# SyncE issues three of a band's sixteen window loads instead of two

## The chip, the cores and the metric

The kernel runs on one core of one Trainium2 chip. The metric is the device time of one execution in microseconds, the median of several. The profile is of one execution of the same kernel, and its span (first to last instruction) is a little shorter than that execution's own time.

## The reference: what is computed

The input is 32 images of 256 channels, 32 x 32 pixels, in f32. Two layers follow one another, each adding its result to its input:

- Layer 0: group norm over 32 groups of 8 channels; values and weights brought to a 16-bit float format; a 3 x 3 convolution from 256 to 256 channels; its result brought to the same format; a bias.
- Layer 1, an "involution": group norm `g = gn(x)` again; a 1 x 1 convolution of g to 64 channels, batch norm and relu; a second 1 x 1 convolution of the result to 16 x 49 values a pixel. These are weights: for each of 16 groups of 16 channels and each pixel, the output is the sum over a 7 x 7 window of g, each place weighted by that pixel's own weight for that place.

```
w = einsum('oc,bchw->bohw', w2, y) + b2      # 784 weights a pixel
out = einsum('bgkhw,bgckhw->bgchw', w, patches)   # k runs over 7 x 7 places
x = x + out
```

## The kernel before

**Tiling.** Images go through one after the other. The work of an image in layer 1 is cut into K = 4 bands of TR = 8 rows; so there are 128 bands. A band has two sides (left and right half of the columns). Instead of gathering the window of each output pixel, the kernel scatters each input pixel: a matrix with one row for each input pixel of the band and one column for each place of an output that it reaches, multiplied with the pixels' channels, adds all outputs of the window in PSUM. That matrix is banded, which gives `band` its name: three tiles (NBAND = 3) of 128 partitions, used in turn, zero outside the band. Partition p of the tile holds, for one row and one column pair, 7 columns of 160 weights.

**How a band comes about** (all in f32):

1. `weights` (L403): matmuls on PE (L411) make the 784 weights of 4 rows of pixels into PSUM tiles `pw`; DVE adds the bias and writes them to the ring `w_sb` (L435).
2. `scatter` (L465): SyncE stores the weights of a band to a DRAM tensor `wd` in the shape that the loads need, seven transfers of 160 KB (L476), one for each column of the window: four in a first part, three in a second.
3. `load_bands` (L478): the band is read from `wd` in sixteen transfers (L497), one for each column pair j (column j of the left half and its mirror image of the right half). Each writes 8 partitions (j, j + 16, ...) and two sides, so 16 rows. A row is 7 x 160 + 8 elements, 4,512 bytes; pairs 0, 1 and 2 lie at the edge of the image, where `cut` = 3, 2 and 1 columns of the window fall outside, and have rows of 2,592, 3,232 and 3,872 bytes (40.5, 50.5 and 60.5 KB a transfer, the others 70.5).
4. `sums` (L508): 128 matmuls a band on PE (L522), 64 a side, into `acc`; DVE adds the result to the image (L538), and SyncE stores it (L543).

Beside this, `front` (L284) works on a later image: group norms on ACT and DVE, the 3 x 3 convolution on PE (L332) with its eviction on DVE (L346, L348), the 1 x 1 convolution (L377) and the transposes of the pixels (L396). SyncE also loads the images (L106).

**Order.** The order is written out by hand: a loop over steps n (L556), 16 steps an image, 4 a band. At each step it calls the pieces that are due: `sums` of a side every second step; `weights` 18 steps before the sums of their image's place (LEAD); the two parts of `scatter` one and two steps after the weights that complete a band; `load_bands` 9 steps before the band's first sums. Each engine runs its instructions in that order.

**Two queues.** In `load_bands`, line L496 picks the engine that issues a transfer: SyncE for the pairs in BY_SYNC (L66), GpSimd for all others. ORDER (L67) gives the order of the sixteen. SyncE's queue thus holds, in order: seven scatters a band, two of the band's loads (in most bands between the first and the second part of a scatter), two stores and two image loads an image. GpSimd's queue holds nothing but the other fourteen loads of each band, after some memsets at the start. The first load of a band on each queue waits until the sums of the band that last used this tile (three bands before) are done, and until the scatter has landed in `wd`. Each queue uses eight DMA semaphores in turn, and a transfer waits for the one that used its semaphore last, that is, the eighth before it.

Of the kernel before, what the change touches and what calls it, by code (L numbers as in the profile page):

```python
# [62 lines left out]
ROW = S * WPIX  # L63
WR = 4
NBAND = 3
BY_SYNC = (0, 1)  # L66
ORDER = (0, 4, 8, 12, 2, 5, 9, 13, 3, 1, 6, 10, 14, 7, 11, 15)  # L67
NPIX = 6
RING = 32
# [9 lines left out]
def tile_quant_conv_then_involution(  # L79
# [398 lines left out]
    def load_bands(b, k):  # L478
# [3 lines left out]
        for i, j in enumerate(ORDER):  # L482
# [12 lines left out]
            )  # L495
            queue = nc.sync if j in BY_SYNC else nc.gpsimd  # L496
            queue.dma_start(to, src)  # L497
# [140 lines left out]
```

## Time and profile before

| | before |
|---|---|
| three timed runs | 1355.0, 1355.05, 1357.66 us; median 1355.05 |
| the profiled execution | 1344.24 us, its span 1342.5 us |
| PE busy | 1253.6 us (93%) |
| GpSimd busy | 1014.4 us (76%), 980.3 of it in 1,792 band loads of 0.549 us |
| SyncE's band loads | 256 |
| DMA, mean rate | 270 GB/s, 361.85 MB |
| queue of SyncE | 229.38 MB, 56.8% of 16 engines |
| queue of GpSimd | 128.28 MB, 33.9% of 16 engines |
| mean granted clock of TensorE | 0.982 |

How to read it: "busy" is the time in which an engine works on instructions; for GpSimd the issue of a DMA counts, since it writes the descriptors itself; for SyncE no issue counts as busy. A wait row tells which engine and line stood idle, what it was released by, the total in us, the number of times and the longest. A wait that ends with a DMA is for its landing. "issue" is a wait for nothing that the profile shows. Where the text speaks of records, it is of the single instructions, semaphore counts and DMA packets of the same trace: a transfer's landing is the last count on its semaphore before that semaphore is used again.

### The profile page before, as it was taken

The page shows a single profiled execution, that of the slowest core. Times are in us where ns is not written, and L with a number is a line of the kernel's source. Part 1 is how long each engine was busy: PE and PEld are TensorE (multiplying, and loading weights), DVE is VectorE, ACT ScalarE, POOL GpSimd, SP SyncE. Part 2 cuts the span into 40 slices and gives each one's busy share as a digit, 9 for nine tenths or more (in the row PEclk, how much of TensorE's full clock was granted, in tenths as well). Part 3 has the DMA queues.
Part 4 walks back from the last instruction along what each step waited for, and adds up shares of the span by engine and source line. Part 5 has one row for each costly group of instructions (what it writes and reads, how often), then busy time and mean ns, then how long its engine had stood idle before and what let it go on. Part 6 is the DMA issues. An engine that isn't in the chain of part 4 may idle for free.

```text
span 1342.5 us, 65799 instructions
## 1 busy us (share of the span) xinstructions
PE 1253.6 (93%) x27648; PEld 763.7 (57%) x27648; DVE 818.8 (61%) x2539; ACT 733.3 (55%) x1731; POOL 1014.4 (76%) x1818
## 2 busy tenths in 40 slices
PE   5899999999999999999999999999999999999665
PEld 2356566565555655556655556666555566556454
DVE  3466666565666665656665666766666666666442
ACT  5775656455656556556545655655556564553300
POOL 9067878777787778777778787788777877788785
PEclk9999999999999999999999999999999999999987
DMA  6089999999999999999999999999999999999995
GB/s 228 11 237 295 271 293 293 279 266 281 272 286 282 291 285 270 283 263 280 293 282 283 270 288 282 293 297 296 281 288 275 277 284 290 271 281 266 278 274 166
DMA packets 360724, 361.85 MB, mean 270 GB/s; under 512 B 75056, under 2 KB 304752, under 8 KB 359152
## 3 DMA queue, kind: packets, MB, share of 16 engines
q1 hardware_dynamic: 278512, 229.38, 56.8%
q0 software_dynamic: 81920, 128.28, 33.9%
q8 instruction: 220, 3.60, 1.1%
q14 instruction: 72, 0.59, 0.1%
HBM read 176.60 MB, written 180.76 MB: 266 GB/s over the span
## 4 chain that ended last, share of the span: by engine, by line
PE 60%; DMA 23%; POOL 7%; issue 3%; ACT 3%; DVE 2%; SPq 1%; POOLq 0%; DVEq 0%; ACTq 0%
PE pc L332 25%; PE acc L522 19%; DMA band<-wd 17%; PE pw L411 11%; POOL band L497 7%; DMA wd<-w_sb 6%; PE pt L396 3%; PE py L377 3%; ACT junk L214 1%; SPq L476 1%; DVE w_sb L435 1%; DMA x<-in_x 1%; ACT xn L273 0%; SPq L497 0%; ACT xq L273 0%
## 5 line engine op out<-in xcount | busy, mean ns | idle before, releaser
L497 POOL DMA_DIRECT2D band<-wd x1792 | 980.3, 549 | 315.7 <-DMA band<-wd 182.0
L435 DVE TENSOR_TENSOR w_sb<-pw,late_sb 128x224 f32<-128x224 f32 (+7 forms) x1280 | 330.4, 322 | 419.5 <-PE pw L411 419.2
L332 PE MATMUL pc<-xq,wq 128*128 128x496 f16 (+3 forms) x2304 | 535.2, 379 | 20.3 <-ACT xq L273 18.3
L522 PE MATMUL acc<-band,pixels 64*32 64x190 f32 (+1 forms) x16384 | 426.6, 332 | 51.8 <-DMA band<-wd 42.7
L522 PEld LDWEIGHTS acc<-band,pixels 64*32 64x32 f32 x16384 | 304.7, 107 | 159.7 <-issue 81.1
L332 PEld LDWEIGHTS <-wq 128*128 128x128 f16 x2304 | 206.7, 98 | 316.1 <-issue 102.7
L411 PE MATMUL pw<-late_sb,y 64*32 64x224 f32 (+1 forms) x8192 | 288.9, 333 | 10.8 <-issue 9.4
L538 DVE TENSOR_TENSOR x<-acc,x 128x380 f32<-128x380 f32 (+1 forms) x512 | 262.0, 512 | 32.2 <-PE acc L522 23.2
L411 PEld LDWEIGHTS pw<-late_sb,y 64*32 64x32 f32 x8192 | 186.5, 106 | 38.1 <-issue 21.0
L400 ACT COPY pixels<-pt 128x512 f32<-128x512 f32 x128 | 73.7, 576 | 228.6 <-PE pt L396 228.6
L214 ACT ACTIVATE junk<-x 128x512 f16<-128x512 f32 (+1 forms) x192 | 146.4, 763 | 14.7 <-DVE x L348 12.2
L214 ACT ACTIVATE junk<-x,mean 128x1024 f16<-128x1024 f32 x128 | 147.1, 1149 | 4.3
L245 ACT ACTIVATE s<-back,eps 128x2 f32<-128x2 f32 x64 | 18.9, 296 | 178.6 <-DVE back L230 178.6
L346 DVE TENSOR_SCALAR q<-pc 128x512 f16<-128x512 f32 x128 | 87.2, 681 | 17.6 <-PE pc L332 17.6
L273 ACT ACTIVATE xn<-x,off,rstd 128x512 f32<-128x512 f32 x128 | 96.2, 800 | 0.0
L348 DVE SCALAR_TENSOR_TENSOR x<-q,early_sb,x 128x512 f32<-128x512 f16 x128 | 94.2, 736 | 0.3
L396 PEld LDWEIGHTS pt<-ident,xn 128*128 128x128 f32 x512 | 63.9, 142 | 26.3 <-issue 2.5
L396 PE MATMUL pt<-ident,xn 128*128 128x128 f32 x512 | 78.0, 275 | 0.1
L273 ACT ACTIVATE xq<-x,off,rstd 128x1024 f16<-128x1024 f32 x64 | 75.7, 1227 | 0.0
L235 ACT ACTIVATE mean<-back 128x2 f32<-128x2 f32 x64 | 12.6, 196 | 101.4 <-DVE back L230 101.4
L377 PE MATMUL py<-xn,early_sb 128*64 128x512 f32 x256 | 62.2, 606 | 0.9 <-ACT xn L273 0.9
L224 DVE STREAM_TRANSPOSE across<-sums 128x32 f32<-128x32 f32 x128 | 26.3, 205 | 33.6 <-ACT junk L214 32.4
(40 smaller groups left out, 369.3 us busy)
## 6 DMA issues: line engine op xcount, KB each, us to landing
wd<-w_sb SPq DMA_DIRECT2D x896, 160.0 KB
band<-wd POOLq DMA_DIRECT2D x1664, 70.5 KB, 4.6
x<-in_x SPq DMA_DIRECT2D x64, 512.0 KB
out<-x SPq DMA_DIRECT2D x64, 512.0 KB
band<-wd POOLq DMA_DIRECT2D x128, 60.5 KB, 4.6
band<-wd SPq DMA_DIRECT2D x128, 50.5 KB
band<-wd SPq DMA_DIRECT2D x128, 40.5 KB
band<-in_w SPq DMA_DIRECT2D x2, 1152.0 KB
```

The lines of the kernel that those rows point to most:

```text
L214: nc.scalar.activation(junk[:, n0:n1], src[:, h, n0:n1], func, bias=bias, accum_out=self.sums[:, i : i + 1])
L273: nc.scalar.activation(dst, src, AF.Identity, bias=self.off[:, one], scale=self.rstd[:, one])
L332: nc.tensor.matmul(pc.rearrange("p (r c) -> p r c", c=W)[:, r0 - nt * RT : r1 - nt * RT, c0:c1], wq[:, kh, k, mh * P : (mh + 1) * P], xq[: ...
L346: nc.vector.tensor_scalar(q, pc, F16_MAX, -F16_MAX, ALU.min, ALU.max)
L348: nc.vector.scalar_tensor_tensor(xt[:, mh, cols], q, bias_sb[:, mh : mh + 1], xt[:, mh, cols], ALU.add, ALU.add)
L377: nc.tensor.matmul(py[i * CR : (i + 1) * CR], w1_sb[:, kh, :], px[:, :, i], start=kh == 0, stop=kh == CH - 1,)
L396: nc.tensor.transpose(pt[:, i, h * P : (h + 1) * P], xn[:, h, (m + i) * P : (m + i + 1) * P], ident)
L411: nc.tensor.matmul(pws[i][t * TW : (t + 1) * TW, : dj.stop - dj.start, r], y_sb[b % 2][half, (r0 // 2 + r) * W : (r0 // 2 + r + 1) * W], w ...
L435: nc.vector.tensor_tensor(to, of[:, :, d0:d1], bias[:, :, d0:d1], ALU.add)
L497: queue.dma_start(to, src)
L522: nc.tensor.matmul(at[t * TW : (t + 1) * TW, h, :, f - top : l - top], px[p, a, v * GC : v * GC + TW], of[:, :, a, f - top : l - top, v], ...
L538: nc.vector.tensor_tensor(x_at, of, x_at, ALU.add)
```

## The change

Pair 2 of each band, until now the fourth of GpSimd's fourteen transfers, goes to SyncE's queue. Since ORDER stays as it is, SyncE issues pair 0, pair 2, pair 1 in this order, and GpSimd the thirteen others in the order that they had. Nothing else in the program changes; the same bytes go to the same places.

```
-BY_SYNC = (0, 1)
+BY_SYNC = (0, 1, 2)
 ORDER = (0, 4, 8, 12, 2, 5, 9, 13, 3, 1, 6, 10, 14, 7, 11, 15)
...
             queue = nc.sync if j in BY_SYNC else nc.gpsimd
             queue.dma_start(to, src)
```

More of the change, by code (lines that the diff above doesn't have):

```diff
@@ L65 @@
 NBAND = 3
-BY_SYNC = (0, 1)
+BY_SYNC = (0, 1, 2)
 ORDER = (0, 4, 8, 12, 2, 5, 9, 13, 3, 1, 6, 10, 14, 7, 11, 15)
```

## The prediction

> **What bounds the kernel now.** I read the page from the top, then the waits by engine in two stretches (100 to 1195 us, where all stages run, and 1195 us to the end, where only the last bands are left), then the DMA records one by one. Columns of the first rows: busy us (share of the span) and count; in the group row: busy us, mean ns of one | idle us before, what ended most of it.
>
> ```profile
> PE 1253.6 (93%) x27648; PEld 763.7 (57%) x27648; DVE 818.8 (61%) x2539; ACT 733.3 (55%) x1731; POOL 1014.4 (76%) x1818
> ...
> DMA  6089999999999999999999999999999999999995
> ...
> PE 60%; DMA 23%; POOL 7%; issue 3%; ACT 3%; DVE 2%; SPq 1%; POOLq 0%; DVEq 0%; ACTq 0%
> ...
> L497 POOL DMA_DIRECT2D band<-wd x1792 | 980.3, 549 | 315.7 <-DMA band<-wd 182.0
> ```
>
> PE looks like the bound at 93%, yet a quarter of the chain is DMA and POOL. The group row is the one to take apart: GpSimd spends 0.548 us on each of 14 transfers a band, 7.67 us, and waits for the rest. The waits say for what (us in total, times, longest). First POOL and PE from 100 to 1195 us:
>
> ```profile
> POOL band L497 <- DMA band<-wd: 166.0, 210, 2.9
> POOL band L497 <- issue: 49.4, 65, 3.2
> POOL band L497 <- DMA wd<-w_sb: 21.9, 23, 3.1
> POOL band L497 <- PE acc L522: 3.0, 2, 2.8
> ```
> ```profile
> PE acc L522 <- DMA band<-wd: 13.7, 11, 2.7
> PE pw L411 <- issue: 8.5, 14, 1.1
> PE acc L522 <- issue: 3.6, 5, 1.2
> ```
>
> GpSimd waits mostly for its own earlier transfers. The records show why: its transfers use eight semaphores in turn, and each issue waits until the transfer eight before has landed. Mean time from issue to landing is 4.7 us; eight issues take 4.4 us; so whatever is above that is a stall. It hardly ever waits for a free band (PE acc, 3.0 us). I matched issues, landings and sums band by band (bands 4 to 111): GpSimd starts a band 0.33 us after it ended the one before, but 8.0 us after the band was free and 3.4 us after its scatter had landed; at least 0.63 us always lies between that landing and the start. So **GpSimd is the tight server**: its period is 7.67 busy + 2.2 waiting = 9.9 us, the kernel's own. PE is close behind: its first sums of a band start 1.9 us in the mean after the last transfer has landed, and at 0.16 us when it was waiting.
>
> The other end of the run, 1195 us to the end, the same two engines, and beneath them the busy time by stretch (PE, PEld, DVE, ACT, POOL; then clock, DMA share, GB/s):
>
> ```profile
> PE acc L522 <- DMA band<-wd: 29.0, 11, 4.6
> ```
> ```profile
> POOL band L497 <- DMA band<-wd: 14.3, 25, 1.2
> ```
> ```profile
> 900.00:1100.00 200.00, 194.83 (x4415) 118.62 (x4415) 127.73 (x397) 115.81 (x276) 154.00 (x282) 1.00 0.97 286
> ...
> 1195.00:1330.00 135.00, 104.92 (x2799) 73.83 (x2797) 68.39 (x204) 31.07 (x70) 112.20 (x206) 0.88 0.90 260
> ```
>
> In the last stretch POOL is busy 112 of 135 us, PE 105, and PE waits 29 us for bands: there the run goes at GpSimd's pace. In the steady part PE is busy 1065.9 of the 1095 us (the six stretches of this view), idle 29.1, 13.7 of it by name for bands.
>
> **The change, part by part.** Per band, one GpSimd issue (pair 2, 60.5 KB) goes; SyncE issues it between pairs 0 and 1.
>
> *GpSimd.* Gone: 0.548 us of issue, and its share of the waits for landings. Those are 166.0 us in the steady part's 110 bands, 1.5 a band, 0.11 a transfer. So 0.66 us a band. If the waits stay as they are in all, 0.55; if the unnamed waits go in proportion too (another 49.4/110/14 = 0.03), 0.69. I take 0.66. GpSimd alone would be 128 x 0.66 = 84 us shorter: that is capacity, not gain, since PE is next.
>
> *The last stretch.* GpSimd issues bands 112 to 127 from 1183.3 to 1330.6 us, 9.21 us a band, and the end follows its last issue by 12 us. 16 x 0.66 = **-10.5 us**, little lying beside it, as PE has 30 us free there.
>
> *The steady part.* What is late next is PE. Its waits for bands, 13.7 us in 11 waits, are 1.2 us each; a GpSimd that gains 0.66 us a band up to the 2.8 us (3.4 - 0.63) that the scatter's landing leaves would cover most. Bounds: nothing, if SyncE gives it all back; all of PE's 29.1 us, if the unnamed waits were bands too. I take the named row, **-13.7**.
>
> *SyncE.* A third load of 16 rows of 3,872 bytes. Rows near it: pair 0 takes 0.70 us of issue in the mean (0.58 median), pair 1, next in line behind it, 0.88 (longest 1.58). I take 0.9 a band, as a load behind a load. Behind it on the queue stand pair 1, then in three bands of four the three scatters of the next part (one of which may follow a store), and GpSimd's next band waits for these. In one band of four the x load follows, which waits 2.9 us for a store's landing anyway: free there. SyncE's waits, 100 to 1195 us:
>
> ```profile
> SPq L476 <- DVE w_sb L435: 80.7, 55, 5.1
> SPq L106 <- DMA out<-x: 77.1, 27, 4.1
> SPq L476 <- DMA wd<-w_sb: 34.5, 54, 2.2
> SPq L497 <- DMA wd<-w_sb: 18.1, 31, 1.2
> ```
>
> Waits for DVE and PE, which a longer queue eats before anyone notices, add up to about 147 us (80.7 and some fifteen smaller rows), 1.3 a band; with the x load's free band, 1.5. So 0.9 fits, with 0.6 left. The scatters land up to 0.9 us later, covered by the 2.8 us of mean slack; but a quarter of the bands have under 1.15 us of it. In the 23 bands where GpSimd waits for the scatter today, the way from scatter to sums changes by +0.9 - 0.66 = +0.24 us, 5.5 us. I take **+2** of it, as not all of them reach PE, bounds 0 and +5.5.
>
> *No new wait for the band itself.* Pair 2 needs what pairs 0 and 1 need, and SyncE's last load of a band lands 3.8 to 14.9 us before GpSimd's last (median 9.3), so it isn't the last to come. The eight-in-turn limit holds on SyncE too: 10 issues a band become 11, at 5.2 us to landing 11 x 5.2/8 = 7.2 us of 9.9. The named slot waits (34.5 + 18.1, part of both being other waits on a scatter) would grow by a tenth, 5 us, inside the 0.6 left.
>
> *The DMA engines.* They are full by the digits, but the records overlap on one engine (a 4.5 KB packet takes 174 ns alone, 600 with the other queue's 640-byte packets between), so 97% isn't a limit reached: 40 us stretches run from 258 to 298 GB/s, and the number of GpSimd issues in them goes against their landing time (correlation -0.63), less against the GB/s (-0.37); landing time itself hardly follows the GB/s (+0.28). Pair 2 on GpSimd is 8 packets of 7,744 bytes at 418 ns, 3.3 us of engine time; from 2,592 bytes at 132 ns and 3,232 at 150, 16 packets of 3,872 are some 169 ns each, 2.7 us: a gain of 0.6 in 158 engine-us, 0.4%. Against it: SyncE's loads of 8 partitions signal from eight engines only (18,544 four-byte packets = 16 x 1031 + 8 x 256), so those eight get 0.34 us more each and all lose 0.21: +0.13 us in 9.9. I take nothing for both; bounds -0.4% and +1.3%, -5 and +17 us.
>
> *A rule against it.* The Trainium skill ("DMA: Bandwidth & Descriptors", on why a DMA increments its semaphore by 16) says that a transfer's engine count divides its outermost dimension, and that SyncE's take the lowest-numbered engines; the count of eight agrees with the row above, which engines no run shows. By it all three loads sit on the same half, and the +17 end would be the likelier. The same page, "Issuing engines are not separate DMA queues", grants such a split the issue time alone: 0.55 a band in place of 0.66, 8.8 us in the last stretch in place of 10.5.
>
> **Sum:** -10.5 - 13.7 + 2 = -22 us. The profiled execution took 1344.24 us (span 1342.5, 1.7 around it), so 1322 by its own scale; the median of the three timed runs is 1355.05, 0.8% above, and the same -22 gives **1333**.
>
> **Rivals.**
> 1. *Hidden in the steady part.* PE is busy over 97% there, and its other waits move in when bands come earlier. Only the last stretch is gained: 1355 - 10 = 1345. For it: only 13.7 us by name. Against: images run at 37.8 to 42.4 us each, so some do lose to something.
> 2. *All of PE's gap closes.* The fastest images, 38.0 us with PE at 50.0 of 50, against a mean of 39.7: 27 x 1.7 = 46, and 10 at the end: 1299.
> 3. *It doesn't relieve GpSimd.* Landing times grow with the load on eight engines until its waits take back the 0.66 us: that needs 0.66 x 8/13 = 0.4 us more on 4.7. Time 1355.
> 4. *Slower: SyncE's queue becomes the bound.* Place: the three scatters behind the loads. It decides above 1.5 us of SyncE time a band, its slack. Price: at pair 1's longest, 1.58, plus a third of a slot wait (0.5 us each), 1.75: 0.25 x 110 = 27 us, less the 10 of the end: +17, 1372. For it: issues between 0.30 and 2.64 us show that this queue backs up. Against: the means.
>
> **How the numbers follow.** Likeliest 0.43 (1318 to 1345); rival 1 0.14; rival 2 0.07; rival 3 0.10; rival 4 0.26. Faster by over 0.2% (about what a measurement here can tell): 0.43 + 0.14 + 0.07 = 0.64; same 0.10; slower 0.26. The range runs from 1304, short of rival 2, to 1371, into rival 4 and past the +17 of the eight engines.
>
> **What would show it.** Right: 13 GpSimd issues a band at 0.548; its start after the scatter's landing shrinks from 3.4 us and its waits for the scatter rise; PE's waits for bands fall below 5 us in the steady part and by some 10 at the end; SyncE's wait for DVE w_sb falls from 80.7 towards 10 and its third load takes about 0.9. Wrong: GpSimd's landing time at 5.1 or more (rival 3), SyncE's waits for DVE at zero with issues over 1 us and GpSimd waiting for scatters above 60 us (rival 4).

## The result, and the profile after

The changed kernel takes 1371.12 us (median of four runs, 1369.83 to 1376.16) against 1356.36 us (four runs) before: ratio 1.0128, 95% interval 1.0085 to 1.0170. It is **slower**, by 1.3%, which is some 17 us (15 between the two medians), where 22 us less were forecast. The profiled execution after took 1376.16 us (span 1373.7), 32 more than the profiled one before. The two profiled executions thus lie 2.4% apart, about twice the measured change: differences between their rows tell where the time went, and overstate how much.

The page first: the rows that answer to those shown of the kernel before.

```profile
PE 1254.4 (91%) x27648; PEld 763.9 (56%) x27648; DVE 819.7 (60%) x2539; ACT 735.8 (54%) x1731; POOL 943.1 (69%) x1690
...
DMA  6189989999999999999999999998999999999996
...
PE 65%; DMA 17%; POOL 4%; issue 4%; DVE 3%; SPq 3%; ACT 3%; POOLq 0%; DVEq 0%; ACTq 0%
...
L497 POOL DMA_DIRECT2D band<-wd x1664 | 909.1, 549 | 418.0 <-DMA wd<-w_sb 173.8
```

GpSimd is busy 71 us less, as planned, 128 issues fewer at 0.549 us. But its idle time rose from 316 to 418 us, and what ends most of it has changed: no longer its own transfers (`band<-wd`), but the scatters (`wd<-w_sb`). The waits of GpSimd from 100 to 1195 us (us in total, times, longest) say the same:

```profile
POOL band L497 <- DMA band<-wd: 147.4, 174, 3.1
POOL band L497 <- DMA wd<-w_sb: 123.1, 63, 5.7
POOL band L497 <- issue: 37.0, 54, 2.2
POOL band L497 <- PE pw L411: 12.8, 7, 4.1
POOL band L497 <- PE acc L522: 7.5, 4, 3.7
```

Its waits for its own landings fell by 19 us (166.0 before), its waits for scatters rose by 101 us (21.9 before). PE in the same stretch, then PE and GpSimd from 1195 us to the end:

```profile
PE acc L522 <- DMA band<-wd: 27.1, 17, 3.1
PE acc L522 <- issue: 11.3, 11, 2.5
PE pw L411 <- issue: 9.6, 8, 3.9
```
```profile
PE acc L522 <- DMA band<-wd: 18.4, 6, 4.7
```
```profile
POOL band L497 <- DMA band<-wd: 15.2, 20, 2.1
POOL band L497 <- DMA wd<-w_sb: 11.9, 9, 3.3
```

PE waits for bands twice as long in the steady part as before (13.7) and 11 us less at the end (29.0), where its unnamed waits (`acc` for "issue") rose from 2.5 to 12.0 us; so its waits there are no shorter in all, though this stretch is also some 30 us longer. The busy time by stretch (PE, PEld, DVE, ACT, POOL; clock, DMA share, GB/s) has the share of the DMA engines lower, 0.94 in place of 0.97, and the rate too, 274 in place of 286 GB/s; so nothing here points at a fuller DMA system:

```profile
900.00:1100.00 200.00, 187.91 (x4209) 116.34 (x4211) 124.13 (x386) 112.14 (x265) 138.60 (x254) 0.99 0.94 274
```

And SyncE, 100 to 1195 us:

```profile
SPq L106 <- DMA out<-x: 55.5, 26, 3.6
SPq L476 <- DMA wd<-w_sb: 49.8, 72, 3.2
SPq L497 <- DMA wd<-w_sb: 28.9, 45, 1.4
SPq L476 <- DMA x<-in_x: 20.0, 24, 2.0
SPq L476 <- DVE w_sb L435: 15.7, 26, 3.1
```

Its wait for DVE's weights, the largest of the waits that the prediction counted as slack, is down from 80.7 to 15.7 us; its waits for landings other than the stores' are up. From the records, band by band (bands 4 to 111, means in us; e15 is an experiment below):

| | before | after | e15 |
|---|---|---|---|
| period of GpSimd | 9.92 | 10.25 | 9.90 |
| its issues of one band, waits between them included | 9.59 | 8.75 | 8.69 |
| its gap between bands | 0.33 | 1.49 | 1.19 |
| landing time of its transfers | 4.74 | 4.89 | 4.77 |
| scatter landed to its first issue | 3.38 | 1.58 | 1.38 |
| share of bands in which that is under 0.8 | 12% | 70% | 60% |
| scatter: first part's end to second part's start, median, bands 0 / 1 / 2 / 3 of an image | 2.0 / 2.1 / 2.3 / 0.1 | 3.1 / 2.7 / 3.2 / 0.1 | 1.8 / 1.5 / 2.5 / 0.1 |
| first scatter issue to last landing, the same | 11.6 / 10.5 / 12.7 / 10.4 | 13.2 / 11.6 / 14.5 / 9.8 | 12.0 / 10.5 / 13.0 / 9.6 |
| period in the last 16 bands | 9.21 | 9.01 | 8.78 |

GpSimd gains 0.84 us inside a band and loses 1.16 between bands. The two rows on the scatter show where: SyncE's loads stand between the two parts of the scatter in bands 0 to 2 of an image, and not in band 3. With three of them the second part starts 0.7 to 1.2 us later there, the scatter takes 1.1 to 1.8 us longer from its first issue to its last landing, and GpSimd starts within 0.55 to 0.72 us of its landing (medians, bands 0 to 2). In band 3, where no load stands between, GpSimd still has 4.0 us.

In the mean over bands 0 to 2 a scatter takes 13.08 us from its first issue to its last landing, in place of 11.79. Of the 1.29 us more, 0.46 are the issue of the loads that stand between, 0.25 the scatters' own issue, 0.46 the waits in between, and 0.12 the landing of the last. The profiles of the experiments below agree: 12.5 and 12.8 us in e5 and e7, which also have a third load in this place; 11.8 in e1, e14 and e15, which have two there; 11.2 with one (e4); and 10.9 with none (e3). With pair 2 on ACT, two stand there as well, and it is 12.0 in e2 and e6, 11.8 in e13 and 12.4 in e16.

### The profile page after: what moved, and what is told of

Its sections match the earlier page's. It is cut to its first block, busy times and chain, and to the rows that moved or that the text cites. A ratio compares the mean times of both kernels' runs of the same rounds, so it can differ in the third digit from the quotient of the medians.

```text
span 1373.7 us, 65862 instructions
## 1 busy us (share of the span) xinstructions
PE 1254.4 (91%) x27648; PEld 763.9 (56%) x27648; DVE 819.7 (60%) x2539; ACT 735.8 (54%) x1731; POOL 943.1 (69%) x1690
## 4 chain that ended last, share of the span: by engine, by line
PE 65%; DMA 17%; POOL 4%; issue 4%; DVE 3%; SPq 3%; ACT 3%; POOLq 0%; DVEq 0%; ACTq 0%
PE pc L332 26%; PE acc L522 22%; PE pw L411 12%; DMA band<-wd 12%; DMA wd<-w_sb 5%; POOL band L497 4%; PE py L377 4%; SPq L476 2%; PE pt L396 2%; DVE w_sb L435 2%; ACT junk L214 1%; DMA band<-in_w 1%; DVE x L538 1%; DVE x L348 0%; SPq L497 0%
## 5 line engine op out<-in xcount | busy, mean ns | idle before, releaser
L497 POOL DMA_DIRECT2D band<-wd x1664 | 909.1, 549 | 418.0 <-DMA wd<-w_sb 173.8
L411 PE MATMUL pw<-late_sb,y 64*32 64x224 f32 (+1 forms) x8192 | 288.1, 333 | 12.4 <-issue 11.0
L346 DVE TENSOR_SCALAR q<-pc 128x512 f16<-128x512 f32 x128 | 87.2, 681 | 15.7 <-PE pc L332 15.7
L235 ACT ACTIVATE mean<-back 128x2 f32<-128x2 f32 x64 | 12.7, 198 | 107.5 <-DVE back L230 107.4
L388 ACT ACTIVATE y<-py,bn_shift,bn_scale 128x256 f32<-128x256 f32 x64 | 32.6, 559 | 46.0 <-PE py L377 46.0
## 6 DMA issues: line engine op xcount, KB each, us to landing
band<-wd SPq DMA_DIRECT2D x128, 60.5 KB
```

The costliest lines, as they stand in the source:

```text
L346: nc.vector.tensor_scalar(q, pc, F16_MAX, -F16_MAX, ALU.min, ALU.max)
L411: nc.tensor.matmul(pws[i][t * TW : (t + 1) * TW, : dj.stop - dj.start, r], y_sb[b % 2][half, (r0 // 2 + r) * W : (r0 // 2 + r + 1) * W], w ...
```

## The experiments

Each ratio is to the kernel before on the same chip, with its 95% interval. Line numbers shift by up to three in the edited kernels. A is the theory that the third load delays what stands behind it on SyncE; its rivals are that GpSimd's relief is worth nothing (B), and that 60.5 KB more on eight DMA engines are the price (C).

**e1: pair 2 left out.**

```
         for i, j in enumerate(ORDER):
+            if j == 2:
+                continue
```

> Pair 2 is loaded by nobody (its columns of the result are left out of the computation): GpSimd issues 13 transfers a band, SyncE two, as before the change. It has the relief of GpSimd without the third load on SyncE, and 2.2% fewer bytes. Theory A (the third load makes SyncE's queue, and with it the scatters, late; the relief itself is worth what was predicted): 1335 us, -20; GpSimd's waits for the scatter stay under 60 us in all. Theory B (GpSimd was never the bound, PE and the rest hide its relief): 1345 to 1355. Theory C (what costs time is the load on eight DMA engines): as A here, so it doesn't tell A from C.

Measured 0.9827 (0.9782 to 0.9872), 23 us less. PE's waits for bands in the steady part fall from 13.7 to 0.4 us, the period in the last 16 bands from 9.21 to 8.72. GpSimd, 100 to 1195 us:

```profile
POOL band L499 <- DMA band<-wd: 158.4, 197, 3.0
POOL band L499 <- DMA wd<-w_sb: 71.0, 48, 4.2
```

So there is a gain to be had: B falls. But it moves onto the scatters even here, whose waits triple (the 60 us expected were passed): behind GpSimd the scatter is the next in line.

**e4: one transfer more on GpSimd.**

```
-BY_SYNC = (0, 1)
+BY_SYNC = (0,)
```

> SyncE issues pair 0 alone, GpSimd 15 transfers a band. Theory A: GpSimd was the tight server before, so one transfer more costs about 0.66 us a band: 1355 + 70 to 85 = 1425 to 1440, GpSimd waits for the scatter fall towards 10 us, SyncE waits for DVE w_sb rise over 120. Theory B (GpSimd hidden behind PE): under 1375. If SyncE was already half of the bound with two loads, the price is smaller than 0.66: 1380 to 1420.

Measured 1.0565 (1.0505 to 1.0625), 76 us. The period is 10.55, 0.62 us a band more: what one transfer costs GpSimd, issue and share of the waits. GpSimd's waits for scatters stayed where they were (24.8 us, with 10 expected), but SyncE has time to spare:

```profile
SPq L476 <- DVE w_sb L435: 224.8, 70, 8.1
```

This settles the bound of the kernel before. The two sides differ: one transfer more costs 5.7%, one less, its bytes included, gains 1.7%: the waits for scatters of e1 show one reason, and PE, busy 93% before, is close behind too.

**e2, e6 and e16: pair 2 issued by ACT,** one, three and five steps after the other loads:

```
-            b, i = due(n, 3 - 4 * NBAND)
+            for late in (False, True):      # late: pair 2 alone; STEPS is 1, 3 or 5
+                b, i = due(n, 3 - 4 * NBAND + STEPS * late)
...
-            queue = nc.sync if j in BY_SYNC else nc.gpsimd
+            queue = nc.scalar if j == 2 else nc.sync if j in BY_SYNC else nc.gpsimd
```

> Pair 2 is issued by ACT, one step later than the others, so that GpSimd has 13, SyncE two, and the bytes and the eight engines are those of the changed kernel. Theory A (SyncE's queue order): 1335 to 1345, SyncE waits for DVE w_sb about 80 us as before the change, GpSimd waits for the scatter under 60. Theory C (eight DMA engines): 1365 to 1375 as the changed kernel, landing times of GpSimd at 4.9. What could blur it: ACT's own work waits behind the load; its wait would show on ACT.

> Pair 2 is issued by ACT three steps later than the other loads, when the scatter has long landed, so ACT doesn't wait for it (one step later it waited some 150 us). SyncE has two loads, GpSimd 13, the bytes and the eight engines are those of the changed kernel. If SyncE's queue holds all of the price: ratio 0.98 to 0.988, as without pair 2. If the bytes over eight engines hold what the reordered kernel didn't win: ratio 0.995 to 1.003.

> Pair 2 on ACT, five steps later, so that ACT waits for no scatter (three steps later it still waited 70 us). All of the work is done. If ACT's waiting kept the gain small: 0.983 to 0.992. If pair 2 then is the last load to land and PE waits for it: 1.0 or above, with PE waits for bands over 30 us.

Measured 1.0030 (0.9994 to 1.0066), 0.9954 (0.9914 to 0.9995) and 1.0021 (0.9994 to 1.0049). All three beat the changed kernel's 1.0128 with the same bytes in transfers of the same shape, which speaks against C. None comes near e1. At one step the two signs expected of A didn't come: GpSimd waits 104 us for scatters (under 60 expected) and SyncE 56 for DVE w_sb (about 80). ACT stands waiting for scatters, 132 us ahead of its normalizations (L274), and PE 15 us for those. At three steps ACT waits 70 us for scatters ahead of the pixels' copy, and SyncE's scatters wait 37 us for band loads (2.1 in the changed kernel). These versions trade one engine's wait for another's, and don't isolate the relief. At five steps pair 2 is the last load of its band to land in 32 of 108 bands of the profile (in none at one step, in 2 at three); that may be what holds this version back, but its profiled execution, 1360.47 us, lies 12 us above the median, and nothing tests it.

**e3 and e8: all of SyncE's loads behind the second part of the scatter,** with three of them and with two:

```
+LATE_PAIRS = (0, 1, 2)      # in e8 (0, 1)
...
+            if (j in LATE_PAIRS) != late:
+                continue
...
-            b, i = due(n, 3 - 4 * NBAND)
+            for late in (False, True):
+                b, i = due(n, 3 - 4 * NBAND + late)
```

> SyncE issues all three loads one step later, behind the second part of the next scatter instead of ahead of it. SyncE has the same amount of work as in the changed kernel. Theory A1 (the place ahead of the scatters counts): GpSimd's start no longer sits on the scatter's landing, 1335 to 1350. Theory A2 (the amount of SyncE's work counts, 11 transfers with eight in flight): 1365 to 1375 still, SyncE's waits for DVE w_sb stay under 25 us.

> The kernel before (two loads on SyncE, 14 on GpSimd), with SyncE's two loads one step later, behind the second part of the scatter. If the place matters only because SyncE's queue is overfull with three: ratio 0.998 to 1.003, since GpSimd is the tight server here. If the place is worth 1% by itself in any kernel: 0.987 to 0.992, and the reordered kernel with three loads has still lost something.

Measured 0.9992 (0.9959 to 1.0024) with three and 1.0095 (1.0056 to 1.0134) with two. With three, the later place wins 1.4% and takes back the whole loss, though SyncE has no more slack than in the changed kernel (15.7 us of this row there; 100 to 1195 us):

```profile
SPq L477 <- DVE w_sb L436: 15.0, 31, 1.4
```

So it isn't the amount of SyncE's work, but what stands behind it. With two it costs 1%, which neither theory expected. There GpSimd is the bound, its scatters come sooner than it needs them (4.7 us of slack), and its waits for its own landings rise from 166 to 180 us and its period at the end from 9.21 to 9.63; that the scatters' transfers now come seven in a row and slow its own is argued, not shown.

**e5, e13 and e14: pair 2 with 512 bytes a row in place of 3,872,** on SyncE, on ACT (three steps later) and on GpSimd:

```
-            n = (K1 - cut) * WB + PAD
+            n = (K1 - cut) * WB + PAD if j != 2 else 128
```

> The changed kernel, but SyncE's load of pair 2 fetches 512 bytes a row in place of 3,872 (the rest of pair 2's weights is left out of the computation). Same instruction, same place, same slot among the eight semaphores, an eighth of the bytes. If the instruction and its place and slot are what costs: 1360 to 1372 on the scale where before is 1355 (ratio 1.005 to 1.013). If it is the 60.5 KB on eight engines: as without pair 2, ratio 0.983 to 0.99.

> Pair 2 on ACT, three steps later, with 512 bytes a row in place of 3,872 (the rest of its weights is left out). Beside the full load on ACT (0.995) only the bytes differ; beside pair 2 left out (0.983) only the instruction on ACT. If the bytes made the difference: 0.98 to 0.987. If ACT's issue and waits made it: 0.992 to 0.998.

> The kernel before with 14 transfers on GpSimd, but pair 2's with 512 bytes a row in place of 3,872 (the rest left out). Beside the kernel before only the bytes differ, beside pair 2 left out only one issue of 0.55 us a band on GpSimd. If GpSimd's issue is what the relief was worth: 0.997 to 1.002. If the bytes are: 0.982 to 0.988. The earlier pairs of runs (0.7% and 1.2% for the bytes) put it between, 0.988 to 0.993.

Measured 1.0055 (1.0020 to 1.0089), 0.9920 (0.9891 to 0.9949) and 0.9953 (0.9919 to 0.9988). Without most of its bytes pair 2 is cheaper by 0.7% on SyncE, 0.3% on ACT and 0.5% on GpSimd: some half a per cent wherever it is. Each of these differences is uncertain by 0.4 to 0.6%, so a small surcharge for SyncE's eight landings isn't excluded; but the bytes are far from e1's distance to the changed kernel, 3.0%. That is the end of C as the main cause. Two differences follow. GpSimd's issue by itself is worth 0.9953 - 0.9827 = 1.3% (17 us); the rest of e1's 1.7% were bytes that the change keeps. And an eighth of the bytes in the third load's place still costs 1.0055 - 0.9827 = 2.3%: it is the instruction and its place. Its issue takes as long: 0.85 us in the mean with 512 bytes a row, 0.82 with 3,872 (bands 4 to 111).

**e7: price without relief.**

```
             queue.dma_start(to, src)
+            if j == 2:
+                nc.sync.dma_start(spare[k % 2], src)     # two spare tensors in DRAM; GpSimd keeps its 14
```

> The kernel before, GpSimd with its 14, and SyncE issues a load of pair 2's rows beside it, into a spare place in DRAM, where the changed kernel issues its third load. It has the price on SyncE without the relief on GpSimd (and 2.2% more bytes, written to DRAM). If price and relief add up: the price is 1.013 + 0.017 = 3.0%, ratio 1.025 to 1.035. If the relief was never to be had together with the third load because both sit on the same wait: ratio 1.010 to 1.018, as the changed kernel.

Measured 1.0181 (1.0129 to 1.0232). It lies below the sum, and above the changed kernel by 0.5% with overlapping intervals. So price and relief don't add up: once the scatters are late, what GpSimd saves is spent waiting for them. With 14 issues it waits less than half as long for scatters as with 13 in the changed kernel (123.1), 72 us less, where the issue of 110 loads is 60 us:

```profile
POOL band L498 <- DMA wd<-w_sb: 51.2, 46, 3.8
```

**e9, e10, e11 and e12: image loads later,** in the changed kernel, in the kernel before, in e3 and in e15:

```
-LOAD = -63
+LOAD = -61
```

> The changed kernel, with the loads of the images (two an image on SyncE) issued two steps later, when the store that they wait for has landed; SyncE then doesn't stand still for it (55 us in the steady part, 0.5 us a band). The third load stays in its place, with its bytes and its eight engines. If SyncE's time is what the third load overdrew (0.94 us a band against some 0.86 of slack): ratio 0.985 to 0.998, SyncE waits for DVE w_sb rise again over 40 us, GpSimd waits for the scatter fall under 90. If the price is anything else (bytes, eight engines, the place ahead of the scatters): 1.008 to 1.015 as the changed kernel.

> The kernel before with the same later image loads. GpSimd was the tight server there and SyncE had slack, so SyncE's 77 us of waiting are worth little: ratio 0.995 to 1.002. If SyncE was a bound there too: 0.985 to 0.992.

> All three loads behind the second part of the scatter, and the image loads later: both reliefs of SyncE together. If they add up: 0.0136 from the place and some 0.02 from the time, ratio 0.975 to 0.99. If both give back the same time: 0.99 to 1.0.

> Pairs 0 and 1 in their old place, pair 2 alone behind the second part of the scatter, and the image loads later. In the place of pair 2 the queue often waited for DVE, so this should be the best of the versions with all of the work done: ratio 0.975 to 0.99; as without pair 2, 0.983, if nothing but SyncE's time and place counted. If the bytes of pair 2 over eight engines cost 0.7%, as the thin load suggests: 0.988 to 0.995.

Measured 1.0125 (1.0074 to 1.0177), 1.0170 (1.0122 to 1.0218), 1.0022 (0.9978 to 1.0065) and 0.9986 (0.9951 to 1.0022). The last three lie above all that was expected of them; e9 has the number of its second alternative with nearly the signs of its first (SyncE waits 39.9 us for DVE w_sb, GpSimd 82.4 for scatters). The edit did more than it was meant to. The image loads, two of 512 KB, stood behind the band loads that follow band 3's scatter; now they stand between the two parts of the scatter of band 0, ahead of its loads. The wait for the store went (55.5 to 0.5 us in e9), but from first scatter issue to last landing band 0 takes 16.0 us in e9 in place of 13.2, and 15.2 in e10 in place of 11.8. The scatters now wait for the image loads, which hold two of SyncE's eight semaphores (20.0 us in the changed kernel):

```profile
SPq L476 <- DMA x<-in_x: 87.2, 49, 3.4
```

So they don't test what they were made for. Beside e10, which differs from it by the change alone, e9 shows no price of the third load (1.0125 against 1.0170, intervals overlapping). Why the kernel before loses 1.7% stays open: GpSimd's waits for its own landings rise from 166 to 193 us there, while its waits for scatters fall from 21.9 to 13.4, so it isn't by the same way.

**e15: pair 2 alone behind the second part of the scatter,** pairs 0 and 1 in their place:

```
-            b, i = due(n, 3 - 4 * NBAND)
+            for late in (False, True):      # late: pair 2 alone; else all others
+                b, i = due(n, 3 - 4 * NBAND + late)
```

> Pair 2 on SyncE, one step later than pairs 0 and 1, behind the second part of the scatter; image loads as in the changed kernel. If the place ahead of the scatter's second part is the price: 0.99 to 1.0. If it is the number of SyncE's transfers, wherever they stand: 1.008 to 1.015 as the changed kernel.

Measured 0.9945 (0.9913 to 0.9977). It does all of the work, is **faster than both kernels**, and differs from the changed one by the place of one load in SyncE's queue: 1.8%. The scatter's times are those of before again (third column of the table above), SyncE's waits for landings other than the stores' fall from 103 to 81 us, and GpSimd, 100 to 1195 us, waits less for scatters (123.1 in the changed kernel); the third row is SyncE's slack:

```profile
POOL band L500 <- DMA band<-wd: 162.7, 180, 4.1
POOL band L500 <- DMA wd<-w_sb: 87.8, 54, 5.4
SPq L477 <- DVE w_sb L436: 12.2, 35, 0.9
```

SyncE isn't less loaded: A holds in the form that the place counts. GpSimd still starts at the scatter's landing in 60% of the bands; what differs is when the scatter lands. Pair 2 can afford the later place: SyncE's last load of a band still lands 2.9 us ahead of GpSimd's in the mean, and after it in 4 of 108 bands.

## Why the prediction was wrong

**What bounds the kernel: right.** GpSimd was the tight server, as e4 shows (0.62 us a band for one more; 0.66 was worked out). That PE is next was half of it: the scatter is too.

**GpSimd's relief: right in kind, too large for this change.** The steps gave -10.5 and -13.7 us, 24 in all. Without pair 2 the kernel gains 23 us, of which 6 are bytes that the change keeps and 17 the issue. At the end of the run the period falls by 0.20 us in place of 0.66, 3 us in all; with pair 2 left out 0.49, 8 us.

**SyncE: the step that failed.** It said that the third load takes 0.9 us, that there is 1.5 a band to take it from, so that "0.9 fits, with 0.6 left", and it put +2 us on the path. The three parts, one by one:

- *The 0.9 was about right.* The loads of a band take 2.08 us of issue in place of 1.61, the seven scatters 5.08 in place of 4.89, and the waits for landings other than the stores' rise from 72 to 103 us (100 to 1195 us), 0.3 a band: 1.0 in all.
- *The slack was half.* 147 us of waits for engines were counted as time that a longer queue eats. Only the first row was: `DVE w_sb` fell by 65 us; the small rows beside it were 66 before and 59 after. A row that is put down to the event that came last isn't slack because an engine's name stands in it. With the 22 us that went from the wait for stores, 0.8 us a band was had, and 1.0 was asked. But the shortage alone isn't the price: e15 leaves SyncE as little, with 2.28 us for its loads, and is 1.8% faster. It became one because the scatters stand behind the loads.
- *The cover was a stock, not a flow.* 2.8 us between the scatter's landing and GpSimd's start were set against a delay of 0.9 us. They cover it once. With the scatter of three bands in four 1.29 us longer every time, they are used up, and then GpSimd starts where the scatter lands: in 12% of the bands before, in 70% after. From there on each further delay of the scatter is GpSimd's. The sum charged the delay to the 23 waits for scatters of the kernel before; after the change there are 63. Instead of +2 us on the path, the place cost 1.8% (some 25 us), the distance from e15 to the changed kernel.

The place was named in the slower rival: the scatters behind the loads. Its point of decision, 1.5 us a band, came from the same wrong slack and is nearer to 0.8; its price, +17 us, is what was measured, but by luck: it was worked out from a third load of 1.75 us, which didn't occur. The chance of 0.26 was too small for a queue whose slack had been summed from fifteen rows that weren't followed one by one.

**The signs.** Most of those set for a right prediction came, with a slower kernel: 13 issues, GpSimd's start 1.58 us after the landing in place of 3.4, longer waits for scatters, DVE w_sb at 15.7, a third load of 0.82 us. They are as well what a queue that is too full shows. Only PE's waits for bands in the steady part told the two apart: 27.1 us, where below 5 was set. Of the signs of the slower rival the waits for scatters came (123.1, above 60).

**Right as well:** pair 2 isn't the last to land on SyncE (1.1 us or more ahead of GpSimd's last); landing times stay below 5.1 (4.89), so it isn't the rival of growing landing times; bytes and eight engines cost little. **The rule set against the change** (the Trainium skill, "DMA: Bandwidth & Descriptors", on why a DMA increments its semaphore by 16) would have made the eight engines the price; e5 beside e14, whose transfers count sixteen landings, doesn't show it (0.7% and 0.5% for the bytes). The same page's "Issuing engines are not separate DMA queues", that a split only saves issue time, fits the bytes, which cost about the same on each queue; but one issue less on GpSimd is worth 1.3% here and one transfer more costs 5.7%, and what the move costs is decided by what stands behind it on the queue that takes it.

**Open:** how much of the third load's price in time is its issue and how much the waits that come with it (their shares in the scatter's delay are above, but no run takes the price apart); why moving the image loads alone costs 1.7%; and why the versions on ACT stay behind pair 2 left out by more than its bytes.

## What to carry to other kernels

When work moves from a full queue to one that seems to have time, write out what stands behind its new place and who waits for that; put it behind the transfers on the critical chain, not ahead of them, if it can land later. That is for a queue that backs up: with two loads, where it didn't, the same move cost 1% (e8). Of a queue's waits count only those as slack whose releaser really is the last thing needed, and compare cost and slack per round: a distance between two events covers a delay once, not in every round.

## What the runs showed of the hardware

- The time in which SyncE issues a load hardly follows its bytes: 0.85 us with 16 rows of 512 bytes and 0.82 with 16 rows of 3,872, in the same place of the queue. With it ahead, pair 1's load takes 0.60 in place of 0.91: in these kernels whichever comes second takes the longest.
- Issue on GpSimd is steady, 0.55 us in all versions, and its transfers land in 4.7 to 5.0 us whether GpSimd issues 13, 14 or 15 of them.
- SyncE's loads of eight partitions count eight landings on their semaphore, and one count that comes earlier; GpSimd's loads and the scatters count sixteen landings. That cost nothing that could be measured here: 0.7% for the bytes on SyncE, 0.5% on GpSimd, each within half a per cent.
- A scatter's way from its first issue to its last landing grows with the loads that stand between its parts on SyncE's queue: 10.9 us with none, 11.2 with one, 11.8 with two (up to 12.4 with pair 2 on ACT), 12.5 to 13.1 with three (means of bands 0 to 2, image loads where they were).
